# PSUM tiles of two banks in a ring of four, and passes over both banks, in a softmax-and-lookup convolution block

## The chip, the cores and the metric

The kernel runs on one core of one Trainium2 chip. The metric is the device time of one execution, in microseconds (us). The matmul engine is called PE, and its weight loads, which run beside the matmuls, PEld. ACT is the scalar engine, DVE the vector engine, POOL the third elementwise engine, SP the engine that issues most DMAs. PSUM is the memory that the matmuls write. It has eight banks, and a bank holds 512 fp32 values in each of 128 partitions. ACT and DVE read results out of it.

## What is computed

The input is `x`, 16 images of 256 channels of 28 x 28 pixels in fp32. Each image is first normalized in groups of eight channels. Then come two layers of the same kind, a residual gate and two additions. A layer replaces a 3 x 3 convolution by a lookup: each channel's nine neighbours are compared with 16 learned codes, and a softmax over the 16 distances weighs the rows of a table. Cut to what matters:

```python
def amm_conv3x3(x, centroids, w_sub):
    p = ...                                  # 3x3 patches: [b, n, channel, 9]
    d = sum(p*p) - 2*einsum('bncs,cks->bnck', p, centroids) + sum(centroids**2)
    attn = softmax(-d, axis=-1)              # over 16 codes
    lut = einsum('cks,cso->cko', centroids, w_sub)
    return einsum('bnck,cko->bno', attn, lut)

out = relu(bn1(amm_conv3x3(group_norm(x), centroids1, wsub1)))
out = bn2(amm_conv3x3(out, centroids2, wsub2))
out = relu(se_gate(out) * out + group_norm(x))
return x + out
```

## The kernel before, in words

A *block* is one layer, one image, one half of the input channels and one half of the pixels (14 rows of 28, so 392 columns). There are 2 x 16 x 4 = 128 blocks, each with these steps:

- `logits(u, mm)` for mm = 0 to 3: 16 small matmuls with 32 x 32 weights (`lg`, L357) fill four banks with the distances of 32 channels. Bank i receives four matmuls.
- `exps(u, mm)`: one exponential on ACT for each bank (L369), 392 columns, from PSUM into a tile `e` in SBUF. In the second layer mm = 0 of half of the blocks goes another way: `wide_copy` copies the four banks (L375), and the exponential is taken later in SBUF (L397).
- `num_b(u)`: 32 matmuls (`nb`, L418) into two banks. They give the sums that divide and one row of the weighted codes. `split_b` on ACT and `join_b` on DVE read them, and DVE takes the reciprocal and spreads it (`rb`, L459).
- `num_a(u, mm)` for mm = 0 to 3: eight matmuls each (`na`, L404) into two banks. For mm = 0 and 1 ACT copies each bank to SBUF (`copy_a`, L472) and POOL scales the pair later. For mm = 2 and 3 DVE multiplies each bank by `rb` on its way out (`scale_a`, L478).
- `product`: matmuls with full 128 x 128 weights (`acc`, L486) into one bank. Each pass over one image in one layer has eight such products, of 9, 3, 6, 9, 9, 9, 9 and 9 matmuls (the products of Strassen's scheme, one of them in two parts). POOL forms differences of the operands (L495), and ACT or DVE reads each product once or twice (`acc_copy` L517, `acc_add` L523).

The order on every engine is written by hand: `at(cluster, place, function)` enters a step in a table, and the table is emitted sorted by cluster and place. A block has two clusters, 256 in all. In both, `logits` comes first (two mm, so eight banks). In the even cluster of a block there follow `num_b` of the block before, its first two `num_a`, and a product. In the odd cluster there follow the other two `num_a`, and a product. A product is read at the start of the cluster after it (place 0.0), ahead of that cluster's exponentials.

PSUM is one ring. Every step that needs a result tile takes the next slots of `p_ring`: a slot is one bank and there are eight. The order of taking is fixed with the program: 4 + 4 for `logits`, 2 for `num_b`, 2 for each `num_a`, 1 for a product. A few small matmuls take one slot each: the group statistics of the next image (`gn_mean`, `gn_var`), and the gate (`se_hidden`, `se_gate`). They stand once for every image, right behind a product: in the first layer in the fifth and the sixth cluster of eight by the place of the `logits` that follow them, in the second layer in the seventh and the eighth. The first matmul into a slot waits until the last reader of its contents of eight banks earlier is done. PE runs its queue in order, so what stands behind a waiting load waits too.

Of the kernel before, what the change touches and what calls it, by code (L numbers as in the profile page):

```python
# [8 lines left out]
F32 = mybir.dt.float32  # L9
I32 = mybir.dt.int32  # L10
U32 = mybir.dt.uint32
AF = mybir.ActivationFunctionType
ALU = mybir.AluOpType
AX = mybir.AxisListType
PSUM = bass.MemoryType.PSUM
DRAM = bass.MemoryType.DRAM

P = 128
# [5 lines left out]
N = RT * W  # L24
# [43 lines left out]
def kernel(  # L68
# [20 lines left out]
    nc = tc.nc  # L89
    B, C, _ = x.shape  # L90
# [3 lines left out]
    const = ctx.enter_context(tc.tile_pool(name="const", bufs=1))  # L94
    dram = ctx.enter_context(tc.tile_pool(name="dram", bufs=1, space=DRAM))
    small = ctx.enter_context(tc.tile_pool(name="small", bufs=2))
    p_ring = ctx.enter_context(tc.tile_pool(name="p_ring", bufs=8, space=PSUM))

    gmat = const.tile([P, P], F32, name="gmat")
    make_block_diagonal(nc, gmat, 8)  # L100
    ctx.enter_context(tc.manual_schedule())

    def bank(name):
        return p_ring.tile([P, 512], F32, tag="ps", name=name)

    def view(t, off, dims):
        return bass.AP(t.tensor, t.offset + off, [list(d) for d in dims])
# [154 lines left out]
    def center_add(wf, c0, w, sq):  # L262
        ps = bank("sqp")
        nc.tensor.matmul(ps[:, :w], lhsT=nhalf_sb, rhs=sq[:, :w], start=True, stop=True)
        nc.vector.tensor_add(wf[:, c0 : c0 + w], wf[:, c0 : c0 + w], ps[:, :w])
# [86 lines left out]
    def logits(u, mm):  # L352
        bs = []
        for i in range(4):
            bk = bank("lg")
            for c in range(4):
                nc.tensor.matmul(  # L357
                    bk[32 * c : 32 * c + 32, :N].rearrange("p (r w) -> p r w", w=W),
                    lhsT=wts["wd", u["hh"]][32 * i : 32 * i + 32, mm, c, :],
                    rhs=u["pt", mm // 2][32 * i : 32 * i + 32, 4 * (mm % 2) + c, :].rearrange("p (r w) -> p r w", w=PW)[:, :, :W],  # L360
                    start=True, stop=True,
                )
            bs.append(bk)
        u["lg", mm] = bs

    def exps(u, mm):
        eg = epool.tile([P, 4, N], F32, tag="e", name="e")
        for i, bk in enumerate(u.pop(("lg", mm))):
            nc.scalar.activation(eg[:, i, :], bk[:, :N], AF.Exp, scale=2.0)  # L369
        u["e", mm] = eg  # L370

    def wide_copy(u, mm):
        eg = epool.tile([P, 4, N], F32, tag="e", name="e")
        for i, bk in enumerate(u.pop(("lg", mm))):
            nc.scalar.copy(eg[:, i, :], bk[:, :N])  # L375
        u["e", mm] = eg

    def wide_turn(u, mm):
# [18 lines left out]
        nc.scalar.activation(eg, eg, AF.Exp, scale=2.0)  # L397

    def num_a(u, mm):
        bs = [bank("na") for _ in range(2)]  # L400
        es = u["e", mm]
        for i in range(4):
            for r in range(2):
                nc.tensor.matmul(  # L404
                    bs[r][32 * i : 32 * i + 32, :N],
                    lhsT=wts["cwa", u["hh"]][64 * r : 64 * r + 64, mm, i, :],
                    rhs=es[64 * r : 64 * r + 64, i, :],
                    start=True, stop=True,
                )
        u["na", mm] = bs  # L410

    def num_b(u):
        bs = [bank("nb") for _ in range(2)]
        for mm in range(4):
            es = u["e", mm]
            for i in range(4):
                for r in range(2):
                    nc.tensor.matmul(  # L418
                        bs[r][32 * i : 32 * i + 32, :N],
                        lhsT=wts["cwb", u["hh"]][64 * r : 64 * r + 64, mm, i, :],  # L420
                        rhs=es[64 * r : 64 * r + 64, i, :],
                        start=(mm == 0), stop=(mm == 3),
                    )
        u["nb"] = bs

    def split_b(u):
        b0, _ = u["nb"]
        r = rpool.tile([P, N], F32, tag="r", name="r")
        nc.scalar.activation(r, b0[:, :N], AF.Identity, bias=zero, scale=m_hi)  # L429
        q = qs["one"][u["qi", 4]]  # L430
        nc.scalar.activation(q, b0[:, :N], AF.Identity, bias=zero, scale=m_lo)
        u["r"] = r
        u["q", 8] = q

    def join_b(u):
        _, b1 = u.pop("nb")
        r, q, w = u["r"], u["q", 8], u["w"]
        nc.vector.scalar_tensor_tensor(  # L438
            r, b1[:, :N], m_lo, r, op0=ALU.mult, op1=ALU.add, accum_out=wsum[:, w : w + 1]
        )  # L440
        nc.vector.scalar_tensor_tensor(q, b1[:, :N], m_hi, q, op0=ALU.mult, op1=ALU.add)
# [20 lines left out]
    def pair(u, mm):  # L462
        return qs["pair"][u["qi", mm]]
# [3 lines left out]
        nc.gpsimd.tensor_tensor(q, q, u.pop(("rb", mm)), ALU.mult)  # L467

    def copy_a(u, mm):
        for r, bk in enumerate(u.pop(("na", mm))):  # L470
            u["q", 2 * mm + r] = pair(u, mm)[:, r, :]
            nc.scalar.copy(u["q", 2 * mm + r], bk[:, :N])  # L472

    def scale_a(u, mm):
        rb = u.pop(("rb", mm))
        for r, bk in enumerate(u.pop(("na", mm))):
            u["q", 2 * mm + r] = pair(u, mm)[:, r, :]
            nc.vector.tensor_mul(u["q", 2 * mm + r], bk[:, :N], rb[:, r, :])  # L478

    accs = {}  # L480

# [387 lines left out]
    for j, u in enumerate(blocks):  # L869
# [3 lines left out]
        for p in range(2):  # L873
            u["pt", p] = pts[p]
            at(g + p - NPT, 0.5, patches, u, p, nc.gpsimd if 0 < g + p < 5 else None)
            for q in range(2):
                mm = 2 * p + q
# [179 lines left out]
    with tc.If(rv > 0):  # L1057
        with tc.For_i(0, B, 1) as it:
# [14 lines left out]
            for l in range(2):  # L1073
# [6 lines left out]
                for t2 in range(2):  # L1080
                    us = []
                    for hh in range(2):
                        u = {"l": l, "b": B, "t": t2, "hh": hh, "w": 0}
# [123 lines left out]
```

## Time and profile before

| | before |
|---|---|
| three runs, median (lowest to highest) | 2734.56 us (2731.55 to 2735.21) |
| profiled execution, whole | 2732.52 us |
| its span in the profile | 2731.0 us |
| PE busy | 2663.6 us (98%) |
| weight loads (PEld) | 1293.3 us (47%) |
| DVE busy | 1718.3 us (63%) |
| ACT busy | 1445.9 us (53%) |
| POOL busy | 2075.3 us (76%) |

The span is the stretch from the first to the last recorded instruction. A "busy" PE is one with a matmul under way. Small matmuls run side by side on parts of the array, so the row does not say how full it is. A line of the timeline merges equal instructions that stand together: start, time from first start to last end, engine, line, operands, count, and in brackets how long the engine had been idle and what it waited for. For weight loads "issue" means that nothing in the profile explains the wait.

### The profile page before, as it was taken

How to read it: one execution, taken by the hardware profiler on the slowest of the kernel's cores; microseconds unless marked ns; L12 is line 12 of the kernel's file. 1: busy time of each engine (PE TensorE's matmuls, PEld its weight loads, DVE VectorE, ACT ScalarE, POOL GpSimd, SP SyncE). 2: the span in 40 equal slices, each digit the busy share in tenths (PEclk: the TensorE clock that was granted, in tenths of full speed). 3: DMA queues.
4: the chain of work that ended last, by engine and by line, in shares of the span. 5: the costliest groups of instructions: out<-in, count | busy, mean ns of one | idle time of the engine just before them, and what ended most of it. 6: DMA issues, size and time to landing. Idle time of an engine off the chain costs nothing. (4 is left out here: it accounts for less than half of the span.)

```text
span 2731.0 us, 87796 instructions
## 1 busy us (share of the span) xinstructions
PE 2663.6 (98%) x36984; PEld 1293.3 (47%) x36984; DVE 1718.3 (63%) x3943; ACT 1445.9 (53%) x3233; POOL 2075.3 (76%) x1425
## 2 busy tenths in 40 slices
PE   5899999999999999999999999999999999999998
PEld 2444544444444444444444444444444444444444
DVE  4765655566565556655567766666766676766674
ACT  3445444544445554555545555656556656556653
POOL 4856787766887677876678887788887788887787
PEclk9999999999999999999999999999999999999999
DMA  9665667766566666666585555545555445555441
GB/s 198 150 143 159 144 156 197 190 148 129 151 163 160 172 155 140 172 166 160 127 180 119 106 121 121 115 102 116 115 122 125 111 105 115 115 124 125 110 105 57
DMA packets 223624, 374.50 MB, mean 137 GB/s; under 512 B 30633, under 2 KB 194009, under 8 KB 223225
## 3 DMA queue, kind: packets, MB, share of 16 engines
q1 hardware_dynamic: 216280, 334.87, 53.3%
q0 software_dynamic: 6944, 33.95, 3.7%
q8 instruction: 295, 4.83, 0.8%
q14 instruction: 105, 0.85, 0.1%
HBM read 288.93 MB, written 79.80 MB: 135 GB/s over the span
## 5 line engine op out<-in xcount | busy, mean ns | idle before, releaser
L369 ACT ACTIVATE e<-lg 128x392 f32<-128x392 f32 x1920 | 778.2, 528 | 803.9 <-PE lg L357 797.7
L495 POOL TENSOR_TENSOR qp<-qp,qp 128x784 f32<-128x784 f32 x512 | 938.2, 1861 | 26.0 <-DVE qp L478 26.0
L486 PE MATMUL acc<-qp,w_S 128*128 128x392 f32 x2048 | 704.4, 494 | 0.9 <-POOL qp L495 0.9
L467 POOL TENSOR_TENSOR qp<-qp,rb 128x784 f32<-128x784 f32 x256 | 471.5, 1859 | 181.3 <-DVE rb L459 173.5
L357 PE MATMUL lg<-pt,wd 32*32 32x392 f32 x16384 | 541.2, 504 | 21.1 <-DMA pt<-home 16.2
L459 DVE STREAM_SHUFFLE rb<-r 128x392 f32<-128x392 f32 x1024 | 551.7, 603 | 0.0
L486 PEld LDWEIGHTS acc<-qp,w_S 128*128 128x128 f32 x2048 | 386.7, 190 | 299.1 <-issue 17.4
L486 PE MATMUL acc<-qp,w_A 128*128 128x392 f32 x1536 | 521.2, 492 | 0.0
L438 DVE SCALAR_TENSOR_TENSOR r<-nb,kst,r 128x392 f32<-128x392 f32 x128 | 79.8, 624 | 572.9 <-ACT r L429 557.6
L404 PE MATMUL na<-e,cwa 64*32 64x392 f32 x8192 | 412.1, 495 | 9.0 <-issue 9.0
L486 PEld LDWEIGHTS acc<-qp,w_A 128*128 128x128 f32 x1536 | 291.8, 190 | 213.8
L418 PE MATMUL nb<-e,cwb 64*32 64x392 f32 x8192 | 373.8, 496 | 3.9 <-issue 3.4
L467 POOL TENSOR_TENSOR qo<-qo,rb 128x392 f32<-128x392 f32 x128 | 131.0, 1024 | 301.6 <-DVE rb L455 301.4
L357 PEld LDWEIGHTS lg<-pt,wd 32*32 32x32 f32 x16384 | 232.8, 103 | 257.3 <-issue 170.9
L444 DVE RECIPROCAL r<-r 128x392 f32<-128x392 f32 x128 | 331.9, 2593 | 0.0
L478 DVE TENSOR_TENSOR qp<-na,rb 128x392 f32<-128x392 f32 x512 | 253.3, 554 | 68.4 <-PE na L404 58.9
L404 PEld LDWEIGHTS na<-e,cwa 64*32 64x32 f32 x8192 | 147.0, 106 | 236.4 <-ACT e L369 122.0
L418 PEld LDWEIGHTS nb<-e,cwb 64*32 64x32 f32 x8192 | 144.1, 107 | 226.2 <-issue 140.5
L472 ACT COPY qp<-na 128x392 f32<-128x392 f32 x512 | 211.8, 513 | 9.1 <-PE na L404 9.1
L429 ACT ACTIVATE r<-nb,kst 128x392 f32<-128x392 f32 x128 | 87.6, 684 | 105.6 <-PE nb L418 100.8
L375 ACT COPY e<-lg 128x392 f32<-128x392 f32 x128 | 52.9, 501 | 149.8 <-PE lg L357 149.8
L493 POOL TENSOR_TENSOR qo<-qo,qo 128x392 f32<-128x392 f32 x128 | 130.8, 1022 | 1.7
(149 smaller groups left out, 1747.9 us busy)
## 6 DMA issues: line engine op xcount, KB each, us to landing
pt<-home SPq DMA_DIRECT2D x768, 209.0 KB
pt<-home SPq DMA_DIRECT2D x756, 104.5 KB
home<-xpad SPq DMA_DIRECT2D x31, 899.0 KB
xt<-in_x SPq DMA_DIRECT2D x30, 784.0 KB
out_dram<-y SPq DMA_DIRECT2D x32, 392.0 KB
w_S<-d_wS SPq DMA_DIRECT2D x4, 576.0 KB
st<-in_wsub SPq DMA_DIRECT2D x4, 512.0 KB
st<-d_wa SPq DMA_DIRECT2D x16, 128.0 KB
```

What stands on the lines that cost most here:

```text
L357: nc.tensor.matmul(bk[32 * c : 32 * c + 32, :N].rearrange("p (r w) -> p r w", w=W), lhsT=wts["wd", u["hh"]][32 * i : 32 * i + 32, mm, c, : ...
L369: nc.scalar.activation(eg[:, i, :], bk[:, :N], AF.Exp, scale=2.0)
L404: nc.tensor.matmul(bs[r][32 * i : 32 * i + 32, :N], lhsT=wts["cwa", u["hh"]][64 * r : 64 * r + 64, mm, i, :], rhs=es[64 * r : 64 * r + 64, ...
L418: nc.tensor.matmul(bs[r][32 * i : 32 * i + 32, :N], lhsT=wts["cwb", u["hh"]][64 * r : 64 * r + 64, mm, i, :], rhs=es[64 * r : 64 * r + 64, ...
L444: nc.vector.reciprocal(u["r"], u["r"])
L459: nc.vector.stream_shuffle(rb[:, r, :], u["r"], mask_of(2 * mm + r))
L467: nc.gpsimd.tensor_tensor(q, q, u.pop(("rb", mm)), ALU.mult)
L472: nc.scalar.copy(u["q", 2 * mm + r], bk[:, :N])
L478: nc.vector.tensor_mul(u["q", 2 * mm + r], bk[:, :N], rb[:, r, :])
L486: nc.tensor.matmul(accs[key][:, :N], lhsT=wl[w][:, k, :], rhs=us["q", k], start=first and n == 0, stop=last and n == len(ks) - 1,)
L493: nc.gpsimd.tensor_tensor(out_u["q", 8], in0["q", 8], in1["q", 8], ALU.subtract)
L495: nc.gpsimd.tensor_tensor(pair(out_u, mm), pair(in0, mm), pair(in1, mm), ALU.subtract)
```

## The change

PSUM becomes a ring of four tiles of two banks each. `logits` takes two tiles for each mm, `num_b` and each `num_a` one. A product or a small matmul takes one too and uses its first bank alone. ACT's exponential, `wide_copy` and `copy_a` now read both banks of a tile in one instruction of 2 x 392 columns, and so does DVE's `scale_a`. The matmuls, their order, and the order of all other steps stay as they are.

```diff
--- before.py
+++ after.py
@@ -94,14 +94,17 @@
     const = ctx.enter_context(tc.tile_pool(name="const", bufs=1))
     dram = ctx.enter_context(tc.tile_pool(name="dram", bufs=1, space=DRAM))
     small = ctx.enter_context(tc.tile_pool(name="small", bufs=2))
-    p_ring = ctx.enter_context(tc.tile_pool(name="p_ring", bufs=8, space=PSUM))
+    p_ring = ctx.enter_context(tc.tile_pool(name="p_ring", bufs=4, space=PSUM))
 
     gmat = const.tile([P, P], F32, name="gmat")
     make_block_diagonal(nc, gmat, 8)
     ctx.enter_context(tc.manual_schedule())
 
+    def banks(name):
+        return p_ring.tile([P, 2, 512], F32, tag="ps", name=name)
+
     def bank(name):
-        return p_ring.tile([P, 512], F32, tag="ps", name=name)
+        return banks(name)[:, 0, :]
 
     def view(t, off, dims):
         return bass.AP(t.tensor, t.offset + off, [list(d) for d in dims])
@@ -352,7 +355,9 @@
     def logits(u, mm):
         bs = []
         for i in range(4):
-            bk = bank("lg")
+            if i % 2 == 0:
+                bs.append(banks("lg"))
+            bk = bs[-1][:, i % 2, :]
             for c in range(4):
                 nc.tensor.matmul(
                     bk[32 * c : 32 * c + 32, :N].rearrange("p (r w) -> p r w", w=W),
@@ -360,19 +365,18 @@
                     rhs=u["pt", mm // 2][32 * i : 32 * i + 32, 4 * (mm % 2) + c, :].rearrange("p (r w) -> p r w", w=PW)[:, :, :W],
                     start=True, stop=True,
                 )
-            bs.append(bk)
         u["lg", mm] = bs
 
     def exps(u, mm):
         eg = epool.tile([P, 4, N], F32, tag="e", name="e")
         for i, bk in enumerate(u.pop(("lg", mm))):
-            nc.scalar.activation(eg[:, i, :], bk[:, :N], AF.Exp, scale=2.0)
+            nc.scalar.activation(eg[:, 2 * i : 2 * i + 2, :], bk[:, :, :N], AF.Exp, scale=2.0)
         u["e", mm] = eg
 
     def wide_copy(u, mm):
         eg = epool.tile([P, 4, N], F32, tag="e", name="e")
         for i, bk in enumerate(u.pop(("lg", mm))):
-            nc.scalar.copy(eg[:, i, :], bk[:, :N])
+            nc.scalar.copy(eg[:, 2 * i : 2 * i + 2, :], bk[:, :, :N])
         u["e", mm] = eg
 
     def wide_turn(u, mm):
@@ -397,12 +401,12 @@
         nc.scalar.activation(eg, eg, AF.Exp, scale=2.0)
 
     def num_a(u, mm):
-        bs = [bank("na") for _ in range(2)]
+        bs = banks("na")
         es = u["e", mm]
         for i in range(4):
             for r in range(2):
                 nc.tensor.matmul(
-                    bs[r][32 * i : 32 * i + 32, :N],
+                    bs[32 * i : 32 * i + 32, r, :N],
                     lhsT=wts["cwa", u["hh"]][64 * r : 64 * r + 64, mm, i, :],
                     rhs=es[64 * r : 64 * r + 64, i, :],
                     start=True, stop=True,
@@ -410,13 +414,13 @@
         u["na", mm] = bs
 
     def num_b(u):
-        bs = [bank("nb") for _ in range(2)]
+        bs = banks("nb")
         for mm in range(4):
             es = u["e", mm]
             for i in range(4):
                 for r in range(2):
                     nc.tensor.matmul(
-                        bs[r][32 * i : 32 * i + 32, :N],
+                        bs[32 * i : 32 * i + 32, r, :N],
                         lhsT=wts["cwb", u["hh"]][64 * r : 64 * r + 64, mm, i, :],
                         rhs=es[64 * r : 64 * r + 64, i, :],
                         start=(mm == 0), stop=(mm == 3),
@@ -424,7 +428,7 @@
         u["nb"] = bs
 
     def split_b(u):
-        b0, _ = u["nb"]
+        b0 = u["nb"][:, 0]
         r = rpool.tile([P, N], F32, tag="r", name="r")
         nc.scalar.activation(r, b0[:, :N], AF.Identity, bias=zero, scale=m_hi)
         q = qs["one"][u["qi", 4]]
@@ -433,7 +437,7 @@
         u["q", 8] = q
 
     def join_b(u):
-        _, b1 = u.pop("nb")
+        b1 = u.pop("nb")[:, 1]
         r, q, w = u["r"], u["q", 8], u["w"]
         nc.vector.scalar_tensor_tensor(
             r, b1[:, :N], m_lo, r, op0=ALU.mult, op1=ALU.add, accum_out=wsum[:, w : w + 1]
@@ -467,15 +471,15 @@
         nc.gpsimd.tensor_tensor(q, q, u.pop(("rb", mm)), ALU.mult)
 
     def copy_a(u, mm):
-        for r, bk in enumerate(u.pop(("na", mm))):
+        for r in range(2):
             u["q", 2 * mm + r] = pair(u, mm)[:, r, :]
-            nc.scalar.copy(u["q", 2 * mm + r], bk[:, :N])
+        nc.scalar.copy(pair(u, mm), u.pop(("na", mm))[:, :, :N])
 
     def scale_a(u, mm):
         rb = u.pop(("rb", mm))
-        for r, bk in enumerate(u.pop(("na", mm))):
+        for r in range(2):
             u["q", 2 * mm + r] = pair(u, mm)[:, r, :]
-            nc.vector.tensor_mul(u["q", 2 * mm + r], bk[:, :N], rb[:, r, :])
+        nc.vector.tensor_mul(pair(u, mm), u.pop(("na", mm))[:, :, :N], rb)
 
     accs = {}
```

## The prediction

> **What bounds the kernel now.** I read the page first. PE is busy for 98% of the span, so a change outside PE can only move the end through PE's waits. The exponentials, 128x392 each, are what ACT does most, and ACT is idle for half of the time.
>
> ```profile
> span 2731.0 us, 87796 instructions
> ...
> PE 2663.6 (98%) x36984; PEld 1293.3 (47%) x36984; DVE 1718.3 (63%) x3943; ACT 1445.9 (53%) x3233; POOL 2075.3 (76%) x1425
> ```
>
> The groups by form give the rows that I price passes with: the exponential of one bank, an exponential of 1568 columns, and a pass of ACT over 784 columns, both in SBUF.
>
> ```profile
> L369 ACT ACTIVATE e<-lg 128x392 f32<-128x392 f32 x1920 | 778.2, 528 | 803.9 <-PE lg L357 797.7 <-PE gnp L298 5.4
> ...
> L397 ACT ACTIVATE e<-e 128x1568 f32<-128x1568 f32 x32 | 50.7, 1584 | 0.0
> ...
> L805 ACT ACTIVATE y<-y 128x784 f32<-128x784 f32 x30 | 24.9, 907 | 0.3 <-POOL y L800 0.3
> ```
>
> In the view of waits, PE waits for exponentials 357 times in front of `na`, 122.0 us in all. Most of that is no loss, since the idle time of a weight load covers the last matmuls still running. What is loss I take from two odd clusters in the timeline of weight loads. In the first, `logits` was held up by a late reader and the exponentials had long been done; the second is an ordinary one.
>
> ```profile
> 206.88 0.15 PEld L357 LDWEIGHTS lg<-pt,wd 32*32 32x32 f32 x8 [2.06 <-DVE hpad L523]
> 207.68 0.18 PEld L404 LDWEIGHTS na<-e,cwa 64*32 64x32 f32 x16 [0.64 <-ACT e L369]
> 208.03 0.15 PEld L404 LDWEIGHTS na<-e,cwa 64*32 64x32 f32 x8 [0.17 <-issue]
> 208.36 0.15 PEld L404 LDWEIGHTS na<-e,cwa 64*32 64x32 f32 x8 [0.18 <-issue]
> 209.15 0.30 PEld L486 LDWEIGHTS acc<-qo,w_S 128*128 128x128 f32 x2 [0.64 <-issue]
> ```
>
> ```profile
> 714.48 0.46 PEld L357 LDWEIGHTS lg<-pt,wd 32*32 32x32 f32 x33 [0.56 <-issue]
> 715.17 0.63 PEld L357 LDWEIGHTS lg<-pt,wd 32*32 32x32 f32 x31 [0.23 <-issue]
> 716.43 0.18 PEld L404 LDWEIGHTS na<-e,cwa 64*32 64x32 f32 x16 [0.64 <-ACT e L369]
> 716.80 0.10 PEld L404 LDWEIGHTS na<-e,cwa 64*32 64x32 f32 x1 [0.18 <-ACT e L369]
> 717.12 0.24 PEld L404 LDWEIGHTS na<-e,cwa 64*32 64x32 f32 x15 [0.22 <-issue]
> 718.00 0.19 PEld L486 LDWEIGHTS acc<-qo,w_S 128*128 128x128 f32 x1 [0.64 <-issue]
> ```
>
> ```profile
> 715.47 3.23 ACT L369 ACTIVATE e<-lg 128x392 f32<-128x392 f32 x8 [5.54 <-PE lg L357]
> ```
>
> From the first `na` load to the first product load it takes 209.15 - 207.68 = 1.47 us there and 718.00 - 716.43 = 1.57 here. The 0.10 is the second `na`: its loads split as 1 and 15, because its second bank comes free only with the fourth exponential. Eight exponentials take 3.23 us and the first alone 0.50 (the shortest in this group, by its line), so they follow each other by (3.23 - 0.50)/7 = 0.39, a little less early on, say 0.38. The fourth ends at 715.47 + 3 x 0.38 + 0.50 = 717.11, which is where the fifteen loads start.
>
> **Part one: passes over two banks at the first release.** A pass over 784 columns replaces two over 392. Its length isn't in the trace for PSUM. The rows 0.528 (392) and 1.584 (1568) give 0.35 us for another 392 columns, so 0.50 + 0.35 = 0.85. The row of 784 columns has 0.84 at its shortest and 0.907 as its mean: bounds 0.84 and 0.91. I take 0.85, since it starts from the exponential itself. The pass can start only when its second bank is complete. The first 33 loads go out in 0.46 us, 14 ns each, so four matmuls of two loads each are at most 8 x 14 ns = 0.1 later; they carry less than their own load time, and I take 0.03 (bounds 0 and 0.1).
>
> Pass one then ends at 715.47 + 0.03 + 0.85 = 716.35, before the `na` load of 716.43. Pass two starts 0.38 + 0.35 = 0.73 after the first and ends at 717.08. The undisturbed group has its second `na` at 208.36 - 207.68 = 0.68 after its first, here 717.11. So the split goes, and the product starts 0.10 earlier. Of the eight clusters of a pass over an image, three (second, fourth, sixth) are of this kind, 96 in all: 96 x 0.10 = 9.6 us, of which I take 8. With passes of 0.91 pass one ends at 716.41 and pass two at 715.50 + 0.76 + 0.91 = 717.17, about as late as now: gain 0, or a loss of 0.05 in 256 clusters (13 us) if the completion bound of 0.1 comes on top. In even clusters the first `num_b` has the same release and nothing behind it waits for a second one.
>
> A rule of the Trainium skill puts the pass nearby: the page "ScalarE: Activation LUTs", section "What ACT_TABLE_LOAD costs", gives an ACTIVATE with immediate operands 186 ns plus 0.833 ns a column, with 93 ns of overlap. By that an estimate for 784 columns is 0.84 with the next 0.75 later, pass two would end at 717.09, and the sum would be the same; for 392 it gives 0.51 where the trace has 0.50 to 0.53.
>
> **Part two: fewer waits in `logits`.** The second half of `logits` puts out its 31 loads in 0.63 us, 20 ns each, against 14 in the first half. Before, one matmul in four carries a wait for its bank; after, one in eight (the order of instructions shows it). If the slower pace comes from the four waits in this half, 31 x 6 ns = 0.19 us, two of them are worth 0.09; if from elsewhere, nothing. Pass one's end at 716.35 leaves room for at most 0.08 before it holds `na` itself. I take 0.025 x 256 = 6 us, bounds 0 and 0.08 x 256 = 20.
>
> **Part three: the ring gets shorter.** `logits`, `num_b` and `num_a` take the same banks as before, but a product or small matmul now takes two. In an ordinary cluster the product of the cluster before must be read before the last two banks of `logits` are written, where it was the last one. In the clusters behind a small matmul it lies one tile further back, so that the fifth bank, the start of the second half, waits for it; before it was the seventh. The second layer shows what that meets:
>
> ```profile
> 1514.16 0.46 PEld L357 LDWEIGHTS lg<-pt,wd 32*32 32x32 f32 x33
> ...
> 1514.76 0.46 ACT L517 COPY y<-acc 128x392 f32<-128x392 f32 x1
> ...
> 1514.85 0.63 PEld L357 LDWEIGHTS lg<-pt,wd 32*32 32x32 f32 x31 [0.23 <-issue]
> ```
>
> The copy that reads the product ends at 1515.22, and the second half starts at 1514.85. It will wait 0.37. All later `logits`, `na` and the next product stand behind it on PE. Part of it is made good, since loads that queue up go out at 14 instead of 20 ns (0.19 over the half): net about 0.2. At the gate's second matmul the read ends at 1523.60 and the half starts at 1523.40: 0.2, net 0. In the first layer the product read behind `gn_mean` ends at 746.84 + 0.55 = 747.39, and the half, begun at 746.89, already takes 0.80 instead of 0.63; it will wait 0.5 at its start, net 0.3, against 0.17 now. Behind `gn_var` the read is done 0.81 after the start, 0.12 late: net 0. Together 16 x 0.2 + 15 x 0.13 = 5 us. Two reads of one product, in the third cluster, end after the last bank's turn already, so there the earlier need (one bank, 0.09) counts in 32 clusters: 3 us. I take 8; bounds are 0 and 62 x 0.36 (two banks' time) + 3 = 25.
>
> **Part four: the rest.** ACT has 960 + 64 + 256 fewer instructions and DVE 256 fewer (a bank's DVE pass is 554 ns). A pair of banks takes 0.73 of ACT instead of 0.77, some 50 us of ACT time in all. It lies beside PE, and its cover is large: `copy_a` and `scale_a` end before the next `logits` wants their tiles (the scalings of 1507.24 end at 1509.22, the next `logits` begins at 1514.16). A pair is read as a whole, and both its banks are complete at nearly the same time. I cost it at nothing, bounds -3 and +3.
>
> **The sum.** -8 - 6 + 8 = -6 us. The first layer's even clusters, where ACT runs late after its norms, should get a little of the shorter passes: -1.5. Against the profiled execution that is 2732.5 - 7.5 = 2725. The median of the runs lies 2 us above that execution, so I forecast 2727.
>
> **Rivals.** (1) Slower: a product holds two banks, and `logits` waits for its reader, as in part three. At the bound of 25 us, with gains of at most 9, that gives 2734.6 + 16 = 2750; at a price of 15 and gains of 6, 2744. It decides from the point where a late reader costs all of its 0.36 instead of half. For it: PE has no slack, and the 0.80 us row shows such waits today. Against: 194 of 256 clusters have no small matmul. (The Trainium skill speaks against the change too: "Trainium Kernel Development and Optimization", section "Best Practices", says that consistent bubbles can mean that PSUM ran out. It gives no figure, so it moves no term.)
> (2) No change: passes take 0.91, as the SBUF row has it. Then parts one and two give 0 to 4 and the ring takes 4 to 8: 2735, between 2730 and 2740.
> (3) The loads in `logits` speed up fully and the ring is nearly free: -10 - 13 + 3 = -20, 2715.
> That the change doesn't do what it says I exclude: the instructions stand as passes of 784 columns, in the same order.
>
> **How the numbers follow.** My forecast with case 3 has 0.50, rival 2 0.25, rival 1 0.25. About 0.2%, 5.5 us, is what a measurement of this kernel can tell from no change. Part of rival 2 ends beyond that on either side, so faster is 0.51, the same 0.24, slower 0.25. The likeliest case's own range is 2718 to 2731; the range over the cases is 2712 to 2747.
>
> **What would show it.** Right: exponentials of 128x784 at about 850 ns; in odd clusters `na` loads in groups of 16, 8 and 8 again and 1.47 us from `na` to product; the second half of `logits` below 0.63. Wrong: passes over 880 ns; a new row of `lg` loads waiting for the reader of `acc` (L517, L523) above 10 us; `logits` to `na` longer than 716.43 - 714.48 = 1.95 in ordinary clusters.

## The result and the profile after

The changed kernel takes 2744.95 us in the median of six runs (2738.24 to 2750.76) beside 2734.02 of the kernel before in the same comparison, a ratio of 1.0039 (95% interval 1.0021 to 1.0058). In a second comparison it was 1.0033 (1.0019 to 1.0048; e0 below). So it is slower by some 9 to 11 us, where 7.5 us of gain were forecast (2727 us). All times and ratios leave out two executions that ran far slower than the rest (3363 us in e13 below, 3821 us in the kernel before beside e8). The profiled execution took 2750.76 us, of which the span is:

```profile
span 2749.3 us, 85938 instructions
...
PE 2669.4 (97%) x36984; PEld 1268.4 (46%) x36984; DVE 1696.6 (62%) x3687; ACT 1368.5 (50%) x1953; POOL 2075.1 (75%) x1425
```

ACT is busy 77 us less and DVE 22 us, as intended, and the weight loads 25 us less. PE has 6 us more: part of its matmuls ran at half clock (the mean granted clock is 0.991 of full speed in this execution and 0.995 in that of the kernel before). The groups by form (line, engine, operation, tiles | busy us, mean ns of one | idle us before them, and what ended it) show the passes:

```profile
L373 ACT ACTIVATE e<-lg 128x784 f32<-128x784 f32 x960 | 717.5, 831 | 850.4 <-PE lg L362 848.6
...
L482 DVE TENSOR_TENSOR qp<-na,rb 128x784 f32<-128x784 f32 x256 | 236.9, 962 | 70.3 <-PE na L408 62.1 <-PE acc L490 5.3 <-POOL qp L499 1.3
L476 ACT COPY qp<-na 128x784 f32<-128x784 f32 x256 | 195.9, 823 | 17.5 <-PE na L408 17.5
```

A pass over 784 columns of PSUM takes 831 ns (0.85 was taken). The ordinary odd cluster that the prediction showed at 714.48 stands at 724.46 now. Its weight loads in the timeline, and its passes:

```profile
724.46 0.46 PEld L362 LDWEIGHTS lg<-pt,wd 32*32 32x32 f32 x33 [0.56 <-issue]
725.15 0.58 PEld L362 LDWEIGHTS lg<-pt,wd 32*32 32x32 f32 x31 [0.23 <-issue]
726.39 0.18 PEld L408 LDWEIGHTS na<-e,cwa 64*32 64x32 f32 x16 [0.67 <-ACT e L373]
727.11 0.19 PEld L408 LDWEIGHTS na<-e,cwa 64*32 64x32 f32 x16 [0.53 <-ACT e L373]
727.93 0.30 PEld L490 LDWEIGHTS acc<-qo,w_S 128*128 128x128 f32 x2 [0.64 <-POOL qo L471]
```

```profile
725.52 2.97 ACT L373 ACTIVATE e<-lg 128x784 f32<-128x784 f32 x4 [6.18 <-PE lg L362]
```

The second half of `logits` puts out its 31 loads in 0.58 in place of 0.63. The passes begin 1.06 after the first load, before it was 0.99. The second `na` is now one group of 16, but it waits 0.53 for the second pass. From `na` to the product it takes 1.54, before 1.57. The whole cluster (first `logits` to the next first `logits`) is 0.05 us shorter, 9.59 in place of 9.65. With eight clusters to an image and two layers there are sixteen kinds of cluster, and nine of them are 0.05 us shorter in the median. So the change does gain there. The loss is elsewhere.

Where it is, the timeline of ACT and DVE shows at `split_b` and `join_b`, here in one even cluster of the second layer. Before:

```profile
1580.51 0.73 ACT L429 ACTIVATE r<-nb,kst 128x392 f32<-128x392 f32 x1
1581.07 0.74 ACT L431 ACTIVATE qo<-nb,kst 128x392 f32<-128x392 f32 x1
...
1581.27 0.62 DVE L438 SCALAR_TENSOR_TENSOR r<-nb,kst,r 128x392 f32<-128x392 f32 x1 [6.57 <-ACT r L429]
```

After:

```profile
1596.68 0.69 ACT L433 ACTIVATE r<-nb,kst 128x392 f32<-128x392 f32 x1
1597.24 0.70 ACT L435 ACTIVATE qo<-nb,kst 128x392 f32<-128x392 f32 x1
...
1597.97 0.63 DVE L442 SCALAR_TENSOR_TENSOR r<-nb,kst,r 128x392 f32<-128x392 f32 x1 [6.96 <-ACT qo L435]
```

`split_b` has two activations on ACT, both of the first bank of `nb`. `join_b` reads the second bank on DVE. It began as soon as the first activation was through (0.76 after that one's start). Now it begins after the second (1.29 after). The two banks are one tile, and here the program orders readers of one tile on different engines one behind the other, although they read different banks. Reciprocal (2.59 us), spread, the scaling on POOL, and the indirect DMA that POOL issues behind the scaling are late by the same half microsecond. (The Trainium skill, "PSUM — Partial Sum Buffer", section "PSUM bank collisions raise a hardware error", asks that two engines be kept apart on the same bank and quadrant, and says that different banks run clean. By that rule the added wait isn't needed, and the rows of the kernel before agree: ACT read the first bank from 1581.07 to 1581.81 while DVE read the second from 1581.27 to 1581.89. Taking away the wait alone was not tried.)

PE meets this lateness in two places of an image. In the second layer the sixth cluster (start 1586.22 before, 1602.47 after) wants the product that DVE reads behind the spread. Before:

```profile
1586.22 0.46 PEld L357 LDWEIGHTS lg<-pt,wd 32*32 32x32 f32 x33 [0.56 <-issue]
...
1586.61 0.54 DVE L525 TENSOR_TENSOR y<-y,acc 128x392 f32<-128x392 f32 x1
...
1586.91 0.63 PEld L357 LDWEIGHTS lg<-pt,wd 32*32 32x32 f32 x31 [0.23 <-issue]
```

After:

```profile
1602.47 0.46 PEld L362 LDWEIGHTS lg<-pt,wd 32*32 32x32 f32 x33 [0.56 <-issue]
...
1603.16 0.42 PEld L362 LDWEIGHTS lg<-pt,wd 32*32 32x32 f32 x15 [0.23 <-issue]
...
1603.30 0.54 DVE L529 TENSOR_TENSOR y<-y,acc 128x392 f32<-128x392 f32 x1
...
1603.89 0.18 PEld L362 LDWEIGHTS lg<-pt,wd 32*32 32x32 f32 x16 [0.32 <-DVE y L529]
```

The read begins 0.83 after the cluster in place of 0.39, and the last tile of `logits`, 16 loads, waits for it. This cluster takes 10.06 in place of 9.86. In the first layer it is the seventh cluster: ACT's copy of a product into `hpad` must wait until the indirect DMA has taken the old contents of `hpad`. In the fourth image POOL issues that DMA 10.65 us ahead of the cluster's start in the kernel before and 10.03 ahead in the changed one. The view of waits (engine, tile and line, what ended the wait: us in all, how often, longest), before and then after:

```profile
DVE r L438 <- ACT r L429: 557.6, 94, 9.7
```

```profile
DVE r L442 <- PE na L408: 457.4, 73, 10.9
DVE r L442 <- ACT qo L435: 164.5, 23, 16.2
...
ACT hpad L521 <- DMA home<-hpad,col: 22.1, 5, 7.7
...
PEld lg L362 <- ACT hpad L521: 5.3, 2, 4.0
...
PEld lg L362 <- DVE y L529: 4.4, 14, 0.3
```

The second, third and last of these rows have no counterpart in this profile of the kernel before, and the fourth was 1.7 there. (The first names `na` as what came last; the join does not read it.) The third must be read with care: it varies between profiles. In the profiles of e3, e9 and others below in which the join is not late it reaches 13.4 us, and in those in which it is late it has 13.9 to 27.4. The last row stands only in profiles with a late join. The longest wait of the third row, in the timeline:

```profile
782.65 0.49 ACT L521 COPY hpad<-acc 128x392 f32<-128x392 f32 x1 [7.65 <-DMA home<-hpad,col]
...
783.19 0.23 PEld L362 LDWEIGHTS lg<-pt,wd 32*32 32x32 f32 x16 [3.97 <-ACT hpad L521]
```

A third kind of place is rare. The prediction showed `logits` waiting 2.06 for a late read of `hpad` (206.88). That cluster is the eighteenth of the kernel, number 17 if the first is 0. DVE has extra work there (it ranks the channels for the second layer). After, the wait stands in front of 16 loads, one bank earlier:

```profile
208.95 0.42 PEld L362 LDWEIGHTS lg<-pt,wd 32*32 32x32 f32 x15 [0.23 <-issue]
212.09 0.18 PEld L362 LDWEIGHTS lg<-pt,wd 32*32 32x32 f32 x16 [2.72 <-DVE hpad L527]
```

0.66 longer, and more follows. The view by windows, of the same work behind that wait (us, busy and counts of the engines, then the granted clock of PE, DMA share, GB/s), before and after:

```profile
208.00:211.50 3.50, 3.50 (x39) 1.75 (x24) 3.46 (x11) 0.31 (x1) 0.39 (x1) 1.00 0.59 127
```

```profile
213.20:216.70 3.50, 3.50 (x34) 1.33 (x19) 2.91 (x7) 0.71 (x1) 0.00 (x0) 0.52 0.60 126
```

The clock is at a half for 3.41 us, which costs 1.7 (an estimate, half of that stretch). Together cluster 17 stands 4.31 above the median of its kind, before 2.03.

### The profile page after: what moved, and what is told of

It is laid out like the page before. It is cut to its first block, busy times and chain, and to the rows that moved or that the text cites. A ratio compares the mean times of both kernels' runs of the same rounds, so it can differ in the third digit from the quotient of the medians.

```text
span 2749.3 us, 85938 instructions
## 1 busy us (share of the span) xinstructions
PE 2669.4 (97%) x36984; PEld 1268.4 (46%) x36984; DVE 1696.6 (62%) x3687; ACT 1368.5 (50%) x1953; POOL 2075.1 (75%) x1425
## 4 chain that ended last, share of the span: by engine, by line
PE 92%; DVE 3%; DMA 2%; issue 1%; POOL 1%; SPq 0%; ACT 0%; ACTq 0%; DVEq 0%; POOLq 0%
PE acc L490 48%; PE lg L362 18%; PE na L408 13%; PE nb L422 13%; DMA pt<-home 1%; DVE rb L463 0%; POOL qp L499 0%; DVE r L448 0%; DMA home<-hpad,col 0%; SPq L346 0%; DMA home<-xpad 0%; ACT e L373 0%; DVE c L583 0%; DVE qp L482 0%; DVE gn_dv L308 0%
## 5 line engine op out<-in xcount | busy, mean ns | idle before, releaser
L373 ACT ACTIVATE e<-lg 128x784 f32<-128x784 f32 x960 | 717.5, 831 | 850.4 <-PE lg L362 848.6
L490 PEld LDWEIGHTS acc<-qp,w_S 128*128 128x128 f32 x2048 | 387.4, 191 | 303.2 <-issue 15.5
L362 PEld LDWEIGHTS lg<-pt,wd 32*32 32x32 f32 x16384 | 219.3, 103 | 279.4 <-issue 191.4
L482 DVE TENSOR_TENSOR qp<-na,rb 128x784 f32<-128x784 f32 x256 | 236.9, 962 | 70.3 <-PE na L408 62.1
L408 PEld LDWEIGHTS na<-e,cwa 64*32 64x32 f32 x8192 | 132.3, 106 | 257.6 <-ACT e L373 144.9
L476 ACT COPY qp<-na 128x784 f32<-128x784 f32 x256 | 195.9, 823 | 17.5 <-PE na L408 17.5
L379 ACT COPY e<-lg 128x784 f32<-128x784 f32 x64 | 48.9, 815 | 157.3 <-PE lg L362 157.3
```

Of the source, the lines that this page charges most:

```text
L362: nc.tensor.matmul(bk[32 * c : 32 * c + 32, :N].rearrange("p (r w) -> p r w", w=W), lhsT=wts["wd", u["hh"]][32 * i : 32 * i + 32, mm, c, : ...
L373: nc.scalar.activation(eg[:, 2 * i : 2 * i + 2, :], bk[:, :, :N], AF.Exp, scale=2.0)
L408: nc.tensor.matmul(bs[32 * i : 32 * i + 32, r, :N], lhsT=wts["cwa", u["hh"]][64 * r : 64 * r + 64, mm, i, :], rhs=es[64 * r : 64 * r + 64, ...
L476: nc.scalar.copy(pair(u, mm), u.pop(("na", mm))[:, :, :N])
L482: nc.vector.tensor_mul(pair(u, mm), u.pop(("na", mm))[:, :, :N], rb)
L490: nc.tensor.matmul(accs[key][:, :N], lhsT=wl[w][:, k, :], rhs=us["q", k], start=first and n == 0, stop=last and n == len(ks) - 1,)
```

## The experiments

The theories: A, `join_b` waits for both splits because `nb` is one tile. B, a product holds two banks, so that `logits` misses one. C, passes over two banks release their first bank later. D, the difference is scatter of DMA landings.

**e0: the changed kernel again.**

> The changed kernel once more, for a second profile and as the yardstick of the runs beside it. If its loss is a property of the order of work (theories A, B, C), the ratio to the kernel before is again 1.002 to 1.006, and in its trace the copy of the product into hpad (L521) waits for the indirect DMA in the first layer, about 20 us in all, where the kernel before has no such row. If the loss was scatter of DMA landings (theory D), the ratio is within 0.999 to 1.002 or the row is gone.

1.0033 (1.0019 to 1.0048), and the row of L521 behind the indirect DMA is there again (13.9 us in 3 waits). That row alone decides nothing, since e3, with single banks, has 13.4 in 3. The row of `y` is there again too (4.5 us in 14 waits), and D falls as the sole cause. The medians of the clusters agree with those of the first profile: 9.04 and 9.00 in the seventh of the first layer (before 8.79), 10.06 and 10.05 in the sixth of the second (before 9.86). The seventh scatters between images, from 8.2 to 15.5 in the first profile and from 8.2 to 10.4 in the kernel before (the first two images aside), so its median is rough.

**e1: reciprocal first.** The first join now waits for the first split alone.

```diff
-        at(g + 2, 1.4, split_b, u)     # both activations
-        at(g + 2, 1.5, join_b, u)      # both joins
-        at(g + 2, 1.6, recip_dve, u)
+        at(g + 2, 1.4, split_b, u)     # first activation
+        at(g + 2, 1.41, join_r, u)     # first join
+        at(g + 2, 1.42, recip_dve, u)
+        at(g + 2, 1.46, split_q, u)    # second activation, behind copy_a (1.45)
+        at(g + 2, 1.6, join_q, u)      # second join
```

> The changed kernel, but the reciprocal is issued right behind the first join, which now waits for the first split alone, and the second split (issued behind the two copies of na) and the second join come after it; the same instructions in another order. Theory A (num_b's two banks are one tile, so the first join waits for both splits, and the chain join, reciprocal, spread, scaling on POOL and the indirect DMA behind it runs 0.4 to 0.6 us late): the chain is as early as before, the wait of L521 for the indirect DMA falls from 22 us to below 5, and the time falls by 8 to 16 us, to 0.998 to 1.001 of the kernel before. Theory B (a product holds two banks): no change, 1.003 to 1.005. Theory C (passes over two banks release their first bank later): no change, 1.003 to 1.005.

1.0019 (1.0005 to 1.0033): less than expected, and the row of the copy behind the indirect DMA fell to 9.8 us, not below 5. In the two places it did what A says: the seventh cluster of the first layer fell from 9.02 (the mean of both profiles) to 8.36, the sixth of the second layer from 10.06 to 9.81. The rest is a wait that the order itself makes. `nb` is held until the second join, now behind the reciprocal, and the eighth cluster of the second layer pays 0.67 (8.23 in place of 7.56):

```profile
PEld lg L362 <- DVE qo L451: 23.0, 28, 2.1
```

**e2: the two splits exchanged in the kernel before,** so that the first join must wait for the second activation. Eight single banks, single passes.

```diff
-        nc.scalar.activation(r, b0[:, :N], AF.Identity, bias=zero, scale=m_hi)
         q = qs["one"][u["qi", 4]]
         nc.scalar.activation(q, b0[:, :N], AF.Identity, bias=zero, scale=m_lo)
+        nc.scalar.activation(r, b0[:, :N], AF.Identity, bias=zero, scale=m_hi)
```

> The kernel before, with the two splits of num_b exchanged, so that the first join waits for the second split to run: the suspected wait alone, with eight single banks and passes over one bank. Theory A: 0.4 us late in every block, and a loss of 5 to 15 us, 1.002 to 1.006 of the kernel before, with a row of L517 or its like waiting for the indirect DMA in the first layer. Theories B and C: nothing, 0.999 to 1.001.

1.0064 (1.0044 to 1.0084), some 17 us: the wait alone costs more than the whole change. The same rows come up as in the changed kernel:

```profile
DVE r L438 <- PE na L404: 465.8, 73, 13.2
DVE r L438 <- ACT r L431: 157.5, 22, 9.0
ACT hpad L517 <- DMA home<-hpad,col: 27.4, 6, 6.3
...
PEld lg L357 <- DVE y L525: 4.5, 14, 0.3
```

By the clusters' medians: the seventh of the first layer 9.53 (+0.74, 15 of them, 11 us), the sixth of the second 10.15 (+0.29, 16 of them, 4.7 us). That is more than the changed kernel loses there; why, no run shows. With e1, and e8 to e11 below, A is shown as one cause.

**e3: an unused bank beside each product, in the kernel before.**

```diff
             accs[key] = bank("acc")
+            bank("spare")
```

> The kernel before, with each product taking a second bank of the ring that nothing uses: the ring as short as in the changed kernel's products (small matmuls still take one), all passes over one bank. Theory A: next to nothing, 1.000 to 1.001, as the readings of the changed kernel's clusters behind small matmuls say. Theory B: the whole loss or more, since the gains of the passes are absent, 1.003 to 1.008. Theory C: nothing.

1.0008 (0.9997 to 1.0019), but this tells nothing of B. Nothing writes or reads the bank, so it was free again at once, and PE's loads carry as many waits as in the kernel before (4272). What is left of it is a second look at the kernel before.

**e4: as e1, in three blocks of four;** the third block of an image keeps the old order. **e5: the same order in the kernel before,** the control.

> The changed kernel with the reciprocal in front of the second split and join in three blocks of four; the third block of an image keeps the changed kernel's order, since there the run before showed logits waiting for the late second join. Theory A (join_b waits for both splits): as in that run, the seventh cluster of the first layer takes 8.4 us in place of 9.0 and the sixth of the second layer 9.8 in place of 10.05, and the eighth cluster of the second layer is back from 8.23 to 7.56, so 10 us less than that run: 2724 to 2730, 0.997 to 0.9995 of the kernel before. Theories B and C: the loss stays, 1.002 to 1.004.

> The kernel before with the same order (reciprocal in front of the second split and join in three blocks of four): the control, which says what the order alone is worth without the shared tile. Theory A: the first join does not wait for the second split here, so what is gained is the second join's 0.6 us ahead of the reciprocal: the seventh cluster of the first layer from 8.79 to 8.4, the rest as before, 0.997 to 0.9995 of the kernel before. Then the change itself, without its added wait, is worth the distance from this run to the one of the changed kernel with the same order: about 8 us if the regular gains of 0.05 in four or five clusters of eight are all there is, nothing if theories B or C hold.

e4: 0.9991 (0.9977 to 1.0004), 11 us better than the changed kernel (1.0033). e5: 0.9980 (0.9967 to 0.9992), 5.5 us better than the kernel before. So the new order is worth some 6 us more where the wait was. The eighth cluster is back at 7.56. In e4 the medians of the clusters sum up to 8.6 us less than in e5 (1203.3 + 1299.1 and 1208.1 + 1302.9, behind the tenth cluster). This is what the passes and the fewer waits bring. Yet by the runs e4 is 3 us behind e5, give or take 5. So some 12 us of loss stand against these gains, and A was not all.

**e6: exponentials in single passes, e7: copies and scalings in single passes,** both in the changed kernel.

```diff
-            nc.scalar.activation(eg[:, 2 * i : 2 * i + 2, :], bk[:, :, :N], AF.Exp, scale=2.0)
+            for r in range(2):
+                nc.scalar.activation(eg[:, 2 * i + r, :], bk[:, r, :N], AF.Exp, scale=2.0)
```

> The changed kernel with the exponentials in passes over one bank, all else as in the changed kernel (tiles of two banks, one wait of logits for two banks). It tells the passes from the fewer waits. If the regular gain of 0.054 us in the even-numbered (second, fourth, sixth, eighth) clusters comes from the fewer waits, it stays, and 0.02 to 0.03 of it goes where the second na waits for the pass; the time is 0 to 4 us above the changed kernel's, 1.003 to 1.006. If the passes release their first tile later than single ones do (theory C), this run is faster than the changed kernel, 1.000 to 1.002.

> The changed kernel with copies and scalings of na in passes over one bank, all else as in the changed kernel: 256 more passes each on ACT and DVE, beside PE. Theories A, B and C alike: nothing, 1.002 to 1.005, with the seventh cluster of the first layer within 0.1 of 9.0 us. A loss of over 4 us would say that the longer passes had paid for part of the added wait.

e6: 1.0068 (1.0052 to 1.0083). The odd clusters take 9.72, so 0.13 more than the changed kernel and 0.07 more than the kernel before: a tile of two banks is released by the second of two short passes, later than by one long pass. C falls, and the step is turned round: tiles of two banks lose in these clusters unless the passes are as long. e7: 1.0049 (1.0030 to 1.0069). By the medians it costs 0.12 to 0.15 in the first cluster of an image (12.32 in place of 12.20 in the second layer) and 0.13 in the fifth of the first layer, some 6 us in all, and next to nothing in the others. The time does not tell it from the changed kernel (1.0033).

**e8 to e11: 64 small matmuls ahead of the first `logits`,** in the changed kernel, the kernel before, e4 and e5. In every profile PE stops at some places with nothing that the profile shows to wait for. The DMA queue that the profile calls "instruction" moves packets of 16 KB. In the changed kernel's trace one of them begins at 1864.4, as a stop of PE in cluster 174 begins, and takes 1.2. From 1868.6 PE runs at half clock:

```profile
1867.26 0.14 PEld L408 LDWEIGHTS na<-e,cwa 64*32 64x32 f32 x4 [3.58 <-issue]
```

The page's row of that queue (packets, MB, share of the DMA engines):

```profile
q8 instruction: 295, 4.83, 0.8%
```

That these packets are PE's program is inferred: the traces of e8 to e11, where PE has 128 instructions more, show 296 of them. Theory E holds such stops to be the rest of the loss.

```diff
+    shift = bank("shift")
+    for _ in range(64):
+        nc.tensor.matmul(shift[:32, :2], lhsT=gmat[:32, :32], rhs=gmat[:32, :2], start=True, stop=True)
```

> The changed kernel with 64 small matmuls (32x32 weights, 2 columns, result unused) in PE's idle time before the first logits, so that everything behind stands 128 instructions later in PE's instruction stream; nothing else changes. Theory E (the medians of its clusters sum up to the same as the kernel before's, 2517 us behind the tenth cluster, and the rest of its loss is stalls of PE where a 16 KB block of its instructions lands late, at places that the position of the blocks picks): the stalls of clusters 14 (8.6 to 9 us) and 174 (5.3 us) move or shrink, and the time comes to 0.998 to 1.002 of the kernel before. Theory G (two-bank passes or tiles bring these stalls themselves): they stay where they are, 1.003 to 1.005.

> The kernel before with the same 64 small matmuls: what the position of the blocks is worth there. Theory E: the place of its stalls in the first layer moves, the time changes by up to 8 us either way, 0.997 to 1.003, the sums of the medians of its clusters stay. Theory G: nothing, 0.9995 to 1.0015.

> The changed kernel with the reciprocal first in three blocks of four, and the 64 small matmuls. Its medians sum up to 15 us less than the kernel before's. Theory E: with the stall of cluster 174 and part of that in cluster 14 gone, 2715 to 2724, 0.994 to 0.997 of the kernel before. Theory G: as without the small matmuls, 0.998 to 1.000.

> The kernel before with the reciprocal first in three blocks of four, and the 64 small matmuls. Its medians sum up to 6.4 us less than the kernel before's. Theory E: 0.995 to 1.001, depending on where its blocks fall, and over the two positions together the changed kernel with this order is ahead of it by the 8.6 us of their medians, give or take 4. Theory G: as without the small matmuls, 0.997 to 0.999, and ahead of the changed kernel with this order.

e8: 1.0025 (1.0011 to 1.0039), e9: 0.9999 (0.9987 to 1.0011), e10: 0.9997 (0.9986 to 1.0008), e11: 0.9985 (0.9974 to 0.9997). In the profile of e8 the stop in cluster 174 shrank from 5.3 to 1.7, that in cluster 14 stayed (9.9). The distances between the kernels stayed too: e10 is 0.0012 behind e11, as e4 was 0.0011 behind e5, though the stop in cluster 174 stands 0.9 and 0.0 above the cluster's kind in e10 and e11, 4.3 and 0.4 in e4 and e5. So theory E falls as the sole cause of the difference. As a part it does not fall: that stop is 5.4 and 5.3 in the two profiles of the changed kernel and missing in that of the kernel before, and the times are too wide to tell 4 us.

The runs also bear on A. The reciprocal first takes the seventh cluster of the first layer from 8.58 to 8.19 in the changed kernel (e8, e10), and in the kernel before, where no join was late, it leaves it at 8.24 (e9, e11).

In the traces a steadier difference shows. Clusters 16 and 17 together stand 5.7 to 6.1 above the others of their kind in the eight profiles with tiles of two banks so far (the changed kernel's two, e1, e4, e6, e7, e8, e10); in all eight a stretch of half clock is part of that, some 1.7. With single banks they stand 2.4 to 2.7 above (the kernel before, e2, e3, e5, e11), and 4.0 in e9, where half clock came behind the wait in cluster 17. They wait for a late reader of a product, as in the lines at 212.09. That is B. Cluster 55 waits for a late reader of a small matmul, and there B is small. It stands 3.6 to 3.8 above its kind wherever half clock fell on it, in e2 with single banks too; elsewhere it stands 1.2 to 2.2 above with tiles of two banks, 1.5 with single banks.

**e12: the second bank held in earnest, in the kernel before.** ACT writes two columns into it when the product begins, and the reader of the product reads them.

```diff
             accs[key] = bank("acc")
+            spares[key] = bank("spare")
+            nc.scalar.copy(spares[key][:32, :2], gmat[:32, :2])
...
         nc.scalar.copy(place(l, b, dst), acc_of(l, key))
+        nc.scalar.copy(scrap[:32, :2], spares.pop(key)[:32, :2])
...
         if pop:
+            nc.vector.tensor_copy(scrap[:32, 2:4], spares.pop(key)[:32, :2])
             accs.pop(key)
```

> The kernel before, with each product holding a second bank in earnest: ACT writes two columns into it when the product begins, and the engine that reads the product reads them right behind it. Small matmuls still hold one bank. Theory B (a product's second bank is missing for logits, which shows only where the reader is late): clusters 16 and 17 take 1.2 and 2.3 us longer as in the changed kernel, a stall of over 2 us brings a stretch of half clock of 3.4 us, and the time is 1.001 to 1.003 of the kernel before. Theory C (the loss belongs to the passes): nothing, 0.999 to 1.001.

1.0005 (0.9991 to 1.0019): too wide to tell 0 from 4 us. In its profile the wait came in another form than expected. Cluster 16 stands 7.5 above its kind, since `nb` waits for the spare bank's reader and half clock falls on it, and cluster 17 has no wait:

```profile
197.79 0.23 PEld L418 LDWEIGHTS nb<-e,cwb 64*32 64x32 f32 x16 [4.35 <-DVE scrap L532]
```

So a held bank makes PE wait for a late reader; its price by the time stays open.

**e13 and e14: the readers made early,** in e4 and e5.

```diff
-        at(15 + o, 1.9, rank_make, o)
+        at(16 + o, 0.02, rank_make, o)          # behind the read of the product (0.0)
...
-        at(52 + 2 * part, 2.1, prep_wd3, part)
+        at(52 + 2 * part, 1.95, prep_wd3, part) # its small matmul ahead of the product (2.0)
```

> The changed kernel with the reciprocal first in three blocks of four, and DVE's extra work out of the way of the products: the ranking of channels is issued behind the read of the product, and the small matmul that centres the second layer's weights in front of the product in place of behind it. Theory B: clusters 16, 17 and 55 lose their waits (1.2, 4.3 and 3.7 us above the others of their kind), so 6 to 9 us less than without: 2718 to 2724 beside 2732 of the kernel before, 0.995 to 0.998. Theory C: 0.998 to 1.000, as without.

> The kernel before with the same three moves (reciprocal first in three blocks of four, ranking behind the read, small matmul in front of the product). Its waits in clusters 16, 17 and 55 are 0.4, 2.0 and 1.5 us, so it gains 3 to 4 us over the reciprocal alone: 0.996 to 0.998 of the kernel before. Theory B: the changed kernel with the same moves is then level with it or ahead by up to 5 us, since its regular gains of 8.6 us are no longer given back. Theory C: it stays ahead of the changed kernel.

e13: 0.9973 (0.9960 to 0.9986), e14: 0.9986 (0.9973 to 1.0000). The two moves turn the order of the pair round: the changed kernel is now 0.0013 ahead. e14 missed its expectation: it was to gain 3 to 4 us over e5 and shows none (0.9986 beside 0.9980). Cluster 55 still stands 1.8 above its kind, but clusters 16 and 17 of e13 have no wait left (here 17):

```profile
209.43 0.46 PEld L362 LDWEIGHTS lg<-pt,wd 32*32 32x32 f32 x33 [0.56 <-issue]
210.11 0.58 PEld L362 LDWEIGHTS lg<-pt,wd 32*32 32x32 f32 x31 [0.23 <-issue]
211.36 0.18 PEld L408 LDWEIGHTS na<-e,cwa 64*32 64x32 f32 x16 [0.67 <-ACT e L373]
```

e13 (2722.70 us in the median of its runs beside 2726.96) beats both kernels, though not clearly e5 or e11. Each distance within a pair is no larger than its own uncertainty (some 0.0018), so by the times alone the turn is a hint. The evidence for B is that the waits of clusters 16 and 17 come with the held bank (e12) and go with the late reader (e13). A rival for the turn is the stop of cluster 174: 4.3 in e4 beside 0.4 in e5, but 4.9 and 4.7 in e13 and e14. In e10 and e11 it was nearly gone in both, and the changed kernel was behind by as much as in e4.

## Why the prediction was wrong

The measured 2744.95 us lies 18 us above the forecast of 2727. The sum was -7.5 us; these are its terms.

**Part one** (passes, 8 us) had the mechanism and missed the size. The pass is shorter than taken (0.83), but it starts 0.07 later, not 0.03, since it waits for its second bank. The split of the second `na` went as forecast; in its place the whole second `na` waits for the second pass (groups of 16 and 16, not 16, 8 and 8), so from `na` to the product it takes 1.54, not 1.47: the product comes 0.03 closer, not 0.10.

**Part two** (fewer waits, 6 us) came near. The second half of `logits` is out 0.05 earlier (1.27 after the first load, before 1.32), but the first `na` waits for the first pass and starts only 0.02 earlier (1.93, before 1.95); 0.025 was taken. Parts one and two together are the 8.6 us by which the medians of e4 lie below those of e5; 14 were taken.

**Part three** (8 us lost) came near in size and not in place. Behind the gate's first matmul `logits` was to wait 0.37 for the copy of the product. In the changed kernel's timeline there:

```profile
1531.03 0.10 PEld L362 LDWEIGHTS lg<-pt,wd 32*32 32x32 f32 x1 [0.18 <-ACT se_hid L772]
...
1531.22 0.46 ACT L521 COPY y<-acc 128x392 f32<-128x392 f32 x1
...
1531.31 0.60 PEld L362 LDWEIGHTS lg<-pt,wd 32*32 32x32 f32 x31 [0.17 <-issue]
```

The second half starts while the copy still runs: the third tile is the one that the small matmul's reader gave back, and the product's tile comes after it. So here the tiles come round in the order in which their readers are issued, not in the order in which they were taken, as the description of the ring ahead of the prediction has it. These clusters lose nothing (8.52 in place of 8.55). The loss is in clusters 12, 16, 17 and 55, where a reader on DVE is late: 0.8 + 1.2 + 2.3 + 2.3 = 6.6 us, half clock included. The last 2.3 is mostly half clock, which fell on cluster 55 in e2 too, so B itself accounts for 4 to 6.6.

**Part four** holds the step that failed: "A pair is read as a whole", and "I cost it at nothing, bounds -3 and +3". It priced copies and scalings by their length, and nowhere asked who else waits for a tile that now has two banks. The pair of `num_b` is not read as a whole: it has four readings on two engines, and "nothing behind it waits for a second one" was said of PE only. DVE's first join waits for ACT's second activation and starts 0.5 us later. On PE that comes to some 0.25 us, against what e4 and e5 show without it, in 15 + 16 clusters: some 8 us by the medians. The cover that it named, ACT's and DVE's length beside PE, was there; the start was what counted.

The sum by the runs: -8.6 + 6.6 + 8 = +6 of the 9 us measured in e0 (+4 with the lower price of B). The other 3 to 5 are not settled. The stop in cluster 174 (5.4 and 5.3 us, not there in the kernel before) would be enough, but the traces are of single executions and other such stops differ between them. PE's mean granted clock in the timed runs was 0.9919 in e0 and 0.9933 in the kernel before beside it, which is 4 us, but half clock behind the waits is already part of the terms.

Of the rivals, the first (a product holds two banks, 2744 to 2750) named the time that came, and one of two causes. Its number came right by luck: it put 15 to 25 us on the ring, which cost 4 to 6.6, and knew nothing of the late join. Of the signs of being wrong, passes over 880 ns and more than 1.95 us from `logits` to `na` did not show, and no row of `logits` waiting for a reader of `acc` came above 10 us (5.3, 4.4 and 2.7). The prediction's list had no sign for a wait of DVE. Two small slips in its working change nothing: if passes of 0.85 follow each other by 0.73, those of 0.91 do by 0.79, not 0.76, and with part of rival 2 on the slower side, slower should stand above the 0.25 of rival 1 alone.

## What to carry to other kernels

When two buffers are joined into one, list every reader of both, on every engine, and ask of each what it waits for now: an order by tile can bind readers that never shared a byte, as it did here. Follow the delayed reader's whole chain down to the DMAs queued behind it, since half a microsecond that nothing on its own engine misses came out on PE one or two clusters later. A shorter ring is paid where readers are late, so look for the odd work that makes them late, and move that first.

## What was not expected of the hardware

- The half clock comes after short stops. In the changed kernel's trace PE idle of 2.0 us (until 212.1) and of 1.4 (until 615.5) were each followed by 3.41 us at a half, one of 2.0 (until 885.9) was not. In every trace here the stretches of half clock start whole multiples of 3.413 us apart. The Trainium skill ("TensorE: Matmul & The Clock Gate", Part 1) has a free-running window of 3413 ns, which agrees with both; its rule there, no idle gaps of PE over some 3.4 us, is too lax for what these rows show.
- The seventh cluster of the first layer depends on more than the kernel. Its median is 8.79 in the first profile of the kernel before and 8.24 in e9, e11, e12 and e14. e9 and e11 have the 64 small matmuls, but e12 and e14 do not; these four profiles were taken on another chip than those of e0 to e3. Which of the two it is, or neither, no run here shows.
